# A background planner with other charges, later reads of products, and another split of score units between two engines

## The chip, the core and the metric

The kernel runs on one core of a Trainium2 chip. The core's engines run at the same time and each takes its own instructions in the order in which the program lists them: PE (TensorE, matrix products), DVE (VectorE), ACT (ScalarE), POOL (GpSimd) and SP (SyncE, which here only starts DMA transfers). An engine that reaches an instruction whose input is not ready stands still, and so does everything behind that instruction on the same engine. The metric is the device time of one execution in microseconds (us), lower is better; what is compared is the median of several runs.

## What is computed

One layer of attention with a kernel function of limited reach, then a mixture of experts, each between layer norms, on 4 sequences of 2048 tokens with 256 features, in float32:

```python
# attention: 16 heads of 16; z is one number for each head and token
out_i = sum_j max(0, 1 - |z_i - z_j| / b_h) * v_j          # j over 2048 keys
x = x + layernorm(attention(layernorm(x)) / T)
# experts: 64 experts, the best 8 for each token, at most 128 tokens for an expert
gu = h @ shared_gate_up_w                                   # h = layernorm(x)
shared = silu(gu[:, :512]) * gu[:, 512:] @ shared_down_w * sigmoid(h @ shared_gate_w)
w, idx = top_k(softmax(h @ gate_w), 8)
y = sum over the 8 of  w * (silu(h @ G_e) * (h @ U_e)) @ D_e
x = x + layernorm(y + shared)
```

The reference sorts the z values and uses prefix sums; the kernel forms the sum over j directly, as a matrix product.

## The kernel before

**The foreground** is a loop over 1024 score units (4 batches x 16 heads x 16 key tiles of 128). `score(t)` (L1535) makes one tile `hat` of 128 keys x 2048 queries: the absolute difference of a query row `qb` and a key column `nk`, then the minimum with 1, less 1. The second step is always DVE's (L1553). The first is ACT's (L1549), or, in a unit "on DVE alone", two further DVE instructions (L1544 and L1546). Which it is, is decided while the program is written out, by a running account `spare`: a unit on ACT adds to it, a unit on DVE alone and every background step on DVE subtract, and once it is 1.3 or more the next unit goes to DVE alone. `product(t)` (L1570) multiplies four quarters of the tiles of units t, t-1, t-2 and t-3 with the values on PE (L1579) and accumulates in the PSUM banks `pa`. After that the `hat` buffer is given back; `hat`, `qb` and `ct` share 13 buffers called big.

**The background** is everything else: preparing the next batch's norms, projections and values (`prepare`, L401), the rest of the attention layer, the shared expert and the routing of a finished batch (`finish`, L452), and, from about unit 700, the 64 experts for the tokens of the first two batches (`all_experts`, L980; `expert`, L1022). Each is written as small tasks with an engine, a charge in us, dependencies, and buffers that it takes and puts back. `Background.step` (L82) is called once after each score unit and writes out the tasks that are ready, engine by engine, until the sum of charges reaches that engine's cap for one unit (`CAP`); what was charged over the cap is carried as a debt. A task counts as ready some units after the tasks that it depends on (`LAG`): a DVE task one unit after a PE task, an ACT task four. So the charges, caps and lags set where a background instruction stands between the score units on its engine, and nothing is reordered afterwards.

**An expert** gathers up to 128 tokens (L1026, POOL, from the table `tab_d`), transposes them on PE (L1032), copies them (L1039, DVE), multiplies (L1036, PE), applies Silu (L1043, ACT), multiplies (L1044, DVE), multiplies with the down weights (L1046, PE), scales (L1049, DVE) and scatters with addition (L1051, POOL). Its weights come by two SP transfers (L987, L989) into one of three buffers called half: `h0`, `h1` and one of the ten slots `s0` to `s9`. Its tokens and results lie in a further slot.

**The tail.** After the last unit the planner runs alone (`drain`): the last batch's attention output and routing (`front_last`, `first` L704, `merge`, `ranking` with L1150), the two remaining batches' experts in 15 items (L1204 to L1243), what the loop left of the background, and the final norms of all 16 chunks (`final`, L1277 to L1309). Those finals for the first two batches wait for the last scatter of the first 64 experts.

Of the kernel before, what the change touches and what calls it, by code (L numbers as in the profile page):

```python
# [17 lines left out]
class Task:  # L18
    __slots__ = ("eng", "cost", "fn", "deps", "get", "put", "env", "lat", "at")

    def __init__(self, eng, cost, fn, deps, get, put, env, lat):
        self.eng, self.cost, self.fn, self.deps, self.lat = eng, cost, fn, deps, lat
        self.get, self.put, self.env, self.at = get, put, env, None


class Background:
# [6 lines left out]
    CAP = {"pe": 0.78, "dve": 0.65, "act": 0.30, "pool": 1.5, "sp": 2.0}  # L33
# [15 lines left out]
    def lag(self, d, k):  # L49
        if not self.alone:  # L50
            return self.LAG.get((d.eng, k.eng), 0) if d.lat is None else (d.lat + 3) // 2
        if d.lat is not None:
            return d.lat
        if d.eng == "sp":
            return 0 if k.eng == "sp" else 4
        return 0 if d.eng == k.eng else 1 if d.cost <= 0.7 else 2
# [25 lines left out]
    def step(self):  # L82

        self.t += 1
        full = set()
        cap = dict.fromkeys(self.CAP, 1.0) if self.alone else self.CAP
        for e, c in cap.items():
            self.debt[e] = max(0.0, self.debt[e] - c)
        left = []
        for k in self.q:  # L90
            if k.eng not in full and self.debt[k.eng] >= cap[k.eng]:
                full.add(k.eng)
            if k.eng not in full and self.ready(k, True):
                self.emit(k)
                self.debt[k.eng] += k.cost
            else:
                left.append(k)
        self.q = left
# [41 lines left out]
def sandwich_kernel(ctx: ExitStack, tc: tile.TileContext, x_in, wqT, bq, wkT, bk, wvT, bv, wprojT, log_bw,  # L140
# [84 lines left out]
    with ExitStack() as ph:  # L225
# [14 lines left out]
        def make(tag):  # L240
            uid[0] += 1
            if tag.startswith("s"):
                return sl.tile([P, SLW], F32, tag=tag, name=f"{tag}_{uid[0]}")
            if tag.startswith("pa"):
                return acc.tile([P, BK], F32, tag=tag, name=f"{tag}_{uid[0]}")
            if tag.startswith("h"):
                return wpool.tile([P, T // 2], F32, tag=tag, name=f"{tag}_{uid[0]}")
            if tag.startswith("v"):
                return vp.tile([P, NP, VW], F32, tag=tag, name=f"{tag}_{uid[0]}").rearrange("p a w -> p (a w)")
            if tag.startswith("b"):  # L250
                return bigp.tile([P, T], F32, tag=tag, name=f"{tag}_{uid[0]}")
            return ps.tile([P, BK], F32, tag=tag, name=f"{tag}_{uid[0]}")

        bg = Background(make)
# [32 lines left out]
        def norm_tasks(env, c, src, dst, deps, tag):  # L287

            st = small.tile([P, CH, 6], F32, tag=f"st{tag}{c}", name=f"st{tag}{c}_{uid[0]}")
            mv = small.tile([P, CH, 2], F32, tag=f"mv{tag}{c}", name=f"mv{tag}{c}_{uid[0]}")  # L290
            rs = small.tile([P, CH], F32, tag=f"rs{tag}{c}", name=f"rs{tag}{c}_{uid[0]}")

            def stats(i):
                for j in (i, i + 1):
                    nc.vector.bn_stats(st[:, j, :], src()[:, j, :])

            def scale():
                for j in range(CH):
                    nc.vector.bn_aggr(mv[:, j, :], st[:, j, :])
                nc.vector.tensor_scalar_add(rs, mv[:, :, 1], EPS)  # L300
                nc.gpsimd.tensor_tensor(out=rs, in0=rs, in1=mhalf, op=ALU.pow)  # L301

            def norm(i):
                for j in (i, i + 1):
                    nc.vector.tensor_scalar(dst()[:, j, :], src()[:, j, :], mv[:, j, 0:1], rs[:, j:j + 1],
                                            ALU.subtract, ALU.mult)
            a = [bg.add("dve", 0.75, lambda i=i: stats(i), deps) for i in (0, 2)]
            s = bg.add("dve", 0.6, scale, a)
            w = bg.add("pool", 0.0, lambda: None, [s])
            return [w], norm  # L310

        def transpose_tasks(env, src, dst, deps, key):

            done, reads = [], []
            for k in range(KF):
# [8 lines left out]
                a = bg.add("pe", 0.9, tr, deps, get={kk: "bank"}, env=env)  # L324
                done.append(bg.add("dve", 0.68, ev, [a], put=[kk], env=env))
# [9 lines left out]
        def values(env, c, done, dst, prev=None, b=None):  # L335
# [3 lines left out]
            for i2 in range(2):  # L339
# [17 lines left out]
                m0 = bg.add("pe", 0.95, lambda f=mmv: f(0), done, get={pk: "bank"}, env=env)  # L357
                m1 = bg.add("pe", 0.95, lambda f=mmv: f(1), [m0])
                e0 = bg.add("dve", 0.45, lambda f=evv: f(0), [m0, prev])
                e1 = bg.add("dve", 0.45, lambda f=evv: f(1), [m1, e0], put=[pk], env=env)  # L360
# [40 lines left out]
        def prepare(b, after=(), mdeps=()):  # L401
# [8 lines left out]
            for c in range(NCH):  # L410
# [6 lines left out]
                n_ = [bg.add("dve", 0.85, lambda i=i, f=norm: f(i), w) for i in (0, 2)]  # L417
# [10 lines left out]
            for r in range(R):  # L428
# [5 lines left out]
                for k in range(KF):  # L434
# [11 lines left out]
                    zz = bg.add("pe", 1.1, mmz, xts + [ld, zz], get={pz: "bank"} if zz is None else {}, put=put,  # L446
# [5 lines left out]
        def finish(b, after=()):  # L452
# [6 lines left out]
            def front(c):  # L459
# [15 lines left out]
                for i2 in range(2):  # L475
# [32 lines left out]
                    a = bg.add("pe", 0.9, tr, [free_pc, ld], get={pk: "bank"},  # L508
# [3 lines left out]
                    free_pc = bg.add("dve", 0.85, res, [w, ld], put=[pk], env=env)  # L512
# [4 lines left out]
                n_ = [bg.add("dve", 0.85, lambda i=i, f=norm: f(i), w) for i in (0, 2)]  # L517
# [27 lines left out]
                a = bg.add("pe", 1.4, mml, done, get={pl: "bank"}, env=env)  # L545
# [6 lines left out]
            def shared(c):  # L552
# [7 lines left out]
                for f in range(NI):  # L560
# [12 lines left out]
                    a = bg.add("pe", 1.1, lambda p_=pg, o=f * P, mm=mm: mm(p_, o, 0), done + [a], get=get, env=env)  # L573
                    g1 = bg.add("pe", 1.1, lambda p_=pg, o=f * P, mm=mm: mm(p_, o, 1), [a])
                    a = bg.add("pe", 1.1, lambda p_=pu, o=IS + f * P, mm=mm: mm(p_, o, 0), [g1])
                    a = u1 = bg.add("pe", 1.1, lambda p_=pu, o=IS + f * P, mm=mm: mm(p_, o, 1), [a],
# [3 lines left out]
                    ms.append(bg.add("dve", 0.68, lambda pu=pu, av=av: nc.vector.tensor_tensor(av(), av(), env[pu],  # L580
# [4 lines left out]
                for i2 in range(2):  # L585
# [17 lines left out]
                    a = bg.add("pe", 0.95, lambda f=mmy: f(0), ms + [a], get=get, env=env)  # L603
                    a = bg.add("pe", 0.95, lambda f=mmy: f(1), [a])
                    e0 = bg.add("dve", 0.45, lambda f=evy: f(0), [a, gts])
                    a = bg.add("pe", 0.95, lambda f=mmy: f(2), [a])
                    a = bg.add("pe", 0.95, lambda f=mmy: f(3), [a], put=acts if i2 == 1 else [], env=env)
# [10 lines left out]
            def tail():  # L618
# [29 lines left out]
                for i in range(0, NT, 4):  # L648
                    a = bg.add("dve", 0.6, lambda i=i: rep(i), [a])
# [13 lines left out]
                for r in range(NT // 8):  # L663
# [7 lines left out]
                    t_ = bg.add("pe", 0.9, tr, [a], get={pk: "bank"}, put=["lg"] if r == NT // 8 - 1 else [], env=env)  # L671
# [308 lines left out]
        def all_experts(env, a, half, out):  # L980

            gs = []
            for e in range(E):
                w = ("ew", e)

                def load(e=e, w=w):
# [9 lines left out]
                               [v(0, TW), v(TW, F), v(TW + F, P), v(TW + F + P, F)],  # L996
                               [{es: "slot"}, {}, {}], [[], [], [es]],
# [4 lines left out]
        def early(a, ready):  # L1002

            def bind():
# [8 lines left out]
                bg.free["half"] = [("h0", bg.t), ("h1", bg.t), bg.free["slot"].pop(0)]  # L1013
            env = {}
            a = bg.add("dve", 0.0, bind, [a] + last[B - 1]["v"] + last[B - 1]["z"])
# [6 lines left out]
        def expert(env, e, half, iv, deps, w, gu, dw, wkey, bufs, get, put, wcol):  # L1022
# [15 lines left out]
            a = bg.add("pe", 0.45, tr, [g], get={pt: "bank"}, env=env)  # L1038
            a = bg.add("dve", 0.42, lambda: nc.vector.tensor_copy(xT(), env[pt][:, :F]), [a], get=get[1],  # L1039
                       put=[pt], env=env)  # L1040
            a = bg.add("pe", 0.68, lambda: up(0), [a, w], get={pg: "bank"}, env=env)
            u = bg.add("pe", 0.68, lambda: up(1), [a])
            a = bg.add("act", 0.3, lambda: nc.scalar.activation(sg(), env[pg][:, :P], AF.Silu), [a])  # L1043
            a = bg.add("dve", 0.3, lambda: nc.vector.tensor_tensor(sg(), sg(), env[pg][:, P:2 * P], ALU.mult), [a, u],  # L1044
                       put=[pg], env=env)
            a = bg.add("pe", 0.74, lambda: nc.tensor.matmul(env[po][:, :F], lhsT=sg(), rhs=dw(),  # L1046
                                                           start=True, stop=True), [a], get={po: "bank"},
                       put=put[0] + ([wkey] if wkey else []), env=env)
            a = bg.add("dve", 0.48, lambda: nc.vector.tensor_scalar(og(), env[po][:, :F], wcol(xg()), None, ALU.mult), [a],  # L1049
# [278 lines left out]
        def norm_x0(c):  # L1328
            xv = lambda: chunkview(env0["x", c])
            w, norm = norm_tasks(env0, c, xv, xv, [], "a")  # L1330
            n_ = [bg.add("dve", 0.85, lambda i=i, f=norm: f(i), w) for i in (0, 2)]
            done, reads = transpose_tasks(env0, xv, lambda: featview(env0["xT", c]), n_, ("pt", c))
            bg.add("pe", 0.0, lambda: None, reads, put=[("x", c)], env=env0)
            xt0.append(done)
# [118 lines left out]
        def accumulate(g, r0, nr, k, deps, zz, st):  # L1453

            pz = ("pz", g)
            for r in range(r0, r0 + nr):
# [6 lines left out]
                zz = bg.add("pe", 0.6, mmz, deps + [zz], get={pz: "bank"} if zz is None else {}, env=env0)  # L1463
# [71 lines left out]
        def score(t):  # L1535
# [7 lines left out]
            if spare[0] >= 1.3:  # L1543
# [3 lines left out]
                spare[0] -= 3.7  # L1547
            else:
                nc.scalar.activation(ht, qb[n][0], AF.Abs, bias=k)  # L1549
                spare[0] += 1.92 - 1.23  # L1550
# [4 lines left out]
        def evict(t):  # L1555

            for c in range(4):
                if t - 1 - c >= 0 and (t - 1 - c) % UG == UG - 1:
# [6 lines left out]
                    spare[0] -= 0.7  # L1565
# [24 lines left out]
        with tc.manual_schedule():  # L1590
            for n in range(4):
                load_q(n)
            for t in range(B * NU + 5):
# [27 lines left out]
                if u == 0 and b == B - 2:  # L1621
                    bg.CAP = dict(bg.CAP, pe=0.88, dve=0.8, act=0.4)
# [144 lines left out]
```

## Time and profile before

| | us |
|---|---|
| median of 3 runs | 2415.87 |
| lowest, highest | 2414.73, 2419.77 |
| the profiled execution | 2422.47 |
| its span, first to last instruction | 2420.7 |
| preparation, to the first L1553 | 67.7 |
| 1024 score units, to the end of the last L1553 | 67.7 to 2105.9 |
| tail | 314.8 |

In the profile's groups, a row names the line, the engine, the operation, output and inputs, and the count; then the total busy time, the mean length of one in ns, and the idle time of the engine just before them with what ended it. Two instructions on ACT may overlap at their ends, so busy time divided by count is less than the mean length. In a row of waits the engine and its line stand first, then what it waited for, and then the total in us, the number of times and the longest. Where a table is cut by score stages here, a stage is 64 units, from the start of one L1553 to the start of the 64th after it.

### The profile page before, as it was taken

How to read it: one execution, taken by the hardware profiler on the slowest of the kernel's cores; microseconds unless marked ns; L12 is line 12 of the kernel's file. 1: busy time of each engine (PE TensorE's matmuls, PEld its weight loads, DVE VectorE, ACT ScalarE, POOL GpSimd, SP SyncE). 2: the span in 40 equal slices, each digit the busy share in tenths (PEclk: the TensorE clock that was granted, in tenths of full speed). 3: DMA queues.
4: the chain of work that ended last, by engine and by line, in shares of the span. 5: the costliest groups of instructions: out<-in, count | busy, mean ns of one | idle time of the engine just before them, and what ended most of it. 6: DMA issues, size and time to landing. Idle time of an engine off the chain costs nothing. (4 is left out here: it accounts for less than half of the span.)

```text
span 2420.7 us, 33022 instructions
## 1 busy us (share of the span) xinstructions
PE 1985.7 (82%) x12649; PEld 706.4 (29%) x12649; DVE 1971.5 (81%) x3064; ACT 2012.9 (83%) x1304; POOL 476.4 (20%) x326
## 2 busy tenths in 40 slices
PE   7686888897887888898898978778888878877785
PEld 4231222222222222222322212223233222353643
DVE  4597989998889988999989987878788789878344
ACT  2688999999989999999999999899799899742123
POOL 1000000100002100002100013454434444432432
PEclk9899999999999999999999999999899999998687
DMA  5223352444452312132312033554534443353872
GB/s 162 70 71 100 105 180 64 162 136 153 163 173 90 113 44 83 51 120 85 98 36 79 9 110 84 146 156 105 139 85 112 130 125 88 89 185 123 226 210 73
DMA packets 194871, 274.33 MB, mean 113 GB/s; under 512 B 24624, under 2 KB 165296, under 8 KB 193936
## 3 DMA queue, kind: packets, MB, share of 16 engines
q1 hardware_dynamic: 179536, 248.83, 32.2%
q0 software_dynamic: 15168, 23.31, 5.7%
q8 instruction: 101, 1.65, 0.3%
q14 instruction: 66, 0.54, 0.1%
HBM read 195.47 MB, written 76.61 MB: 112 GB/s over the span
## 5 line engine op out<-in xcount | busy, mean ns | idle before, releaser
L1549 ACT ACTIVATE hat<-qb,nk 128x2048 f32<-128x2048 f32 x978 | 1873.7, 1996 | 116.9 <-DMA qb<-zq_d 61.4
L1579 PE MATMUL pa<-hat,v 128*32 128x512 f32 x8192 | 1116.5, 618 | 327.3 <-DVE hat L1553 317.0
L1553 DVE TENSOR_SCALAR hat<-hat 128x2048 f32<-128x2048 f32 x1024 | 1232.2, 1224 | 118.3 <-ACT hat L1549 113.3
L1579 PEld LDWEIGHTS pa<-hat,v 128*32 128x32 f32 x8192 | 181.5, 109 | 921.5 <-DVE hat L1553 711.7
L1051 POOL DMA_INDIRECT y_d<-s,ix x64 | 154.1, 2407 | 254.3 <-DVE s L1049 173.4
L564 PE MATMUL k<-s,sgu 128*128 128x512 f32 x348 | 196.0, 648 | 0.0
L1026 POOL DMA_INDIRECT s<-tab_d,ix x64 | 113.6, 1775 | 373.4 <-DMA qb<-zq_d 243.5
L301 POOL TENSOR_TENSOR rsa<-rsa,mhalf 128x4 f32<-128x4 f32 x16 | 27.6, 1725 | 579.6 <-DVE rsa L300 562.8
L495 POOL TENSOR_TENSOR rsc<-rsc,mhalf 128x2 f32<-128x2 f32 x24 | 45.7, 1904 | 460.5 <-DVE rsc L494 460.3
L438 PE MATMUL k<-s,s 128*32 128x512 f32 x768 | 103.2, 604 | 0.0
L593 PE MATMUL k<-sd,s 128*128 128x256 f32 x352 | 97.3, 406 | 0.0
L564 PEld LDWEIGHTS k<-s,sgu 128*128 128x128 f32 x348 | 53.8, 192 | 129.4 <-issue 118.1
L593 PEld LDWEIGHTS k<-sd,s 128*128 128x128 f32 x352 | 62.2, 193 | 64.8 <-issue 47.4
L346 PE MATMUL k<-h,s 128*128 128x256 f32 x256 | 74.8, 418 | 0.0
L1036 PEld LDWEIGHTS k<-s,h 128*128 128x128 f32 x360 | 48.4, 201 | 52.7 <-issue 48.9
L704 DVE MAX8 codes<-scT 128x8 f32<-128x1152 f32 (+2 forms) x48 | 63.5, 1323 | 0.2
L346 PEld LDWEIGHTS k<-h,s 128*128 128x128 f32 x256 | 45.3, 196 | 57.8 <-issue 53.9
L1036 PE MATMUL k<-s,h 128*128 128x128 f32 x360 | 59.6, 302 | 2.0 <-issue 2.0
L1296 ACT ACTIVATE b<-b,v 128x256 f32<-128x256 f32 x64 | 33.2, 590 | 33.3 <-DVE v L1291 12.9
L1544 DVE TENSOR_SCALAR hat<-qb,nk 128x2048 f32<-128x2048 f32 x46 | 58.9, 1280 | 0.0
L1546 DVE TENSOR_SCALAR hat<-hat 128x2048 int32<-128x2048 int32 x46 | 56.5, 1228 | 1.6
L706 DVE MATCH_REPLACE8 scT<-codes,scT 128x1152 f32<-128x1152 f32 (+2 forms) x44 | 57.8, 1313 | 0.0
(305 smaller groups left out, 1674.1 us busy)
## 6 DMA issues: line engine op xcount, KB each, us to landing
qb<-zq_d SPq DMA_DIRECT2D x128, 512.0 KB, 6.2
s<-m_d SPq DMA_DIRECT2D x48, 512.0 KB, 4.2
s<-_attn_hidden_states_dram SPq DMA_DIRECT2D x28, 512.0 KB, 5.9
b<-y_d SPq DMA_DIRECT2D x24, 512.0 KB, 7.9
h<-fn_expert_gate_up_w_dram SPq DMA_DIRECT2D x45, 256.0 KB, 3.0
v_d<-h SPq DMA_DIRECT2D x48, 192.0 KB, 1.9
v<-v_d SPq DMA_DIRECT2D x48, 192.0 KB, 2.4
out_dram<-b SPq DMA_DIRECT2D x16, 512.0 KB, 3.9
```

The costliest lines, as they stand in the source:

```text
L346: nc.tensor.matmul(env[pk][:, i * F:(i + 1) * F], lhsT=xv[:, k, o:o + P], rhs=wv[:, k, :], start=(k == 0), stop=(k == KF - 1))
L438: nc.tensor.matmul(env[pz][c * CR:(c + 1) * CR, :], lhsT=xv[:, r, :], rhs=env[mp][:, k * 2 * F:(k + 1) * 2 * F], start=(r == 0 and k == 0) ...
L564: nc.tensor.matmul(env[p_], lhsT=sgu[:, k, o:o + P], rhs=featview(env[xT])[:, k, :], start=(k == 0), stop=(k == KF - 1))
L593: nc.tensor.matmul(env[py][:, i * F:(i + 1) * F], lhsT=env[acts[f // 2]][:, o:o + P], rhs=sd[:, f, :], start=(f == 0), stop=(f == NI - 1))
L704: a = bg.add("dve", 1.25, lambda c8=c8: nc.vector.max(out=c8, in_=scT[:, :w]), ev + [a])
L1026: g = bg.add("pool", 1.3, lambda: nc.gpsimd.indirect_dma_start(out=xg(), out_offset=None, in_=tab_d[half][:, :], in_offset=bass.IndirectOf ...
L1036: nc.tensor.matmul(env[pg][:, m * P:(m + 1) * P], lhsT=gu(k, m), rhs=xT()[:, k * P:(k + 1) * P], start=(k == 0), stop=(k == KF - 1))
L1051: s = bg.add("pool", 1.9, lambda: nc.gpsimd.indirect_dma_start(out=y_d[half][:, :], out_offset=bass.IndirectOffsetOnAxis(ap=iv(), axis=0), ...
L1544: nc.vector.tensor_scalar(ht, qb[n][0], k, None, ALU.add)
L1549: nc.scalar.activation(ht, qb[n][0], AF.Abs, bias=k)
L1553: nc.vector.tensor_scalar(ht, ht, 1.0, 1.0, ALU.min, ALU.subtract)
L1579: nc.tensor.matmul(pa[k, c][32 * j:32 * j + 32, :], lhsT=vt[b, s].rearrange("p a w -> p (a w)")[:, h // 2 * VW + p * D:h // 2 * VW + p * D ...
```

## The change

Six things are edited.

- The charges of many tasks are set to other numbers: transposes on PE go from 0.9 to 0.6 or 0.58, a step of the query and key projection from 1.1 to 0.88, a value product from 0.95 to 1.1, the router's product from 1.4 to 1.9, a down product of the shared expert from 0.95 to 1.07, and so on.
- The caps: PE 0.78 becomes 0.84 for the first two batches; in the last two PE stays at 0.88, and DVE goes from 0.8 to 0.75.
- A task that PE leaves with a debt over 0.65 is marked late, and whatever depends on it is written out one unit later.
- The account of `spare` gets other numbers.
- The tokens and results of one of the 64 early experts lie in half a slot, four halves made of two slots that are taken for good; three of the four small tiles of an expert now lie over one another.
- The buffers for these experts' weights are `h0`, `h1` and two slots that are taken for good, four instead of three.

```diff
-    CAP = {"pe": 0.78, "dve": 0.65, "act": 0.30, "pool": 1.5, "sp": 2.0}
+    CAP = {"pe": 0.84, "dve": 0.65, "act": 0.30, "pool": 1.5, "sp": 2.0}
...
         if not self.alone:
-            return self.LAG.get((d.eng, k.eng), 0) if d.lat is None else (d.lat + 3) // 2
+            return self.LAG.get((d.eng, k.eng), 0) + d.late if d.lat is None else (d.lat + 3) // 2
...
                 self.emit(k)
                 self.debt[k.eng] += k.cost
+                k.late = int(k.eng == "pe" and self.debt["pe"] > 0.65)
...
+            if tag.startswith("e"):
+                return ess[int(tag[1:]) // 2][:, int(tag[1:]) % 2 * (SLW // 2):]
...
+        NES, ess = 4, []
...
-                a = bg.add("pe", 0.9, tr, deps, get={kk: "bank"}, env=env)
-                done.append(bg.add("dve", 0.68, ev, [a], put=[kk], env=env))
+                a = bg.add("pe", 0.6, tr, deps, get={kk: "bank"}, env=env)
+                done.append(bg.add("dve", 0.63, ev, [a], put=[kk], env=env))
...
-                    zz = bg.add("pe", 1.1, mmz, xts + [ld, zz], get={pz: "bank"} if zz is None else {}, put=put,
+                    zz = bg.add("pe", 0.88, mmz, xts + [ld, zz], get={pz: "bank"} if zz is None else {}, put=put,
                                 env=env)
...
                 es = ("es", e)
                 v = lambda o, n, es=es: lambda: env[es][:, o:o + n]
...
-                               [v(0, TW), v(TW, F), v(TW + F, P), v(TW + F + P, F)],
-                               [{es: "slot"}, {}, {}], [[], [], [es]],
+                               [v(0, TW), v(0, F), v(TW, P), v(0, F)], [{es: "es"}, {}, {}], [[], [], [es]],
...
-                bg.free["half"] = [("h0", bg.t), ("h1", bg.t), bg.free["slot"].pop(0)]
+                bg.free["half"] = [("h0", bg.t), ("h1", bg.t), env["tag", "wq"][1:] + (bg.t,), env["tag", "wr"][1:] + (bg.t,)]
+                ess[:] = [env["e", i] for i in range(NES // 2)]
+                bg.free["es"] = [(f"e{i}", bg.t) for i in range(NES)]
             env = {}
-            a = bg.add("dve", 0.0, bind, [a] + last[B - 1]["v"] + last[B - 1]["z"])
+            get = {("e", i): "slot" for i in range(NES // 2)}
+            a = bg.add("dve", 0.0, bind, [a] + last[B - 1]["v"] + last[B - 1]["z"], get=dict(get, wq="slot", wr="slot"), env=env)
...
             if spare[0] >= 1.3:
                 nc.vector.tensor_scalar(ht, qb[n][0], k, None, ALU.add)
                 hi = ht.bitcast(I32)
                 nc.vector.tensor_scalar(hi, hi, 0x7fffffff, None, ALU.bitwise_and)
-                spare[0] -= 3.7
+                spare[0] -= 3.6
             else:
                 nc.scalar.activation(ht, qb[n][0], AF.Abs, bias=k)
-                spare[0] += 1.92 - 1.23
+                spare[0] += 1.9 - 1.17
...
-                    spare[0] -= 0.7
+                    spare[0] -= 0.63
...
-                    bg.CAP = dict(bg.CAP, pe=0.88, dve=0.8, act=0.4)
+                    bg.CAP = dict(bg.CAP, pe=0.88, dve=0.75, act=0.4)
```

The charges that the diff leaves out here, old and new: statistics of a norm 0.75 and 0.67, their scaling 0.6 and 0.47, applying a norm 0.85 and 0.68, a value's eviction 0.45 and 0.35, the first batch's projection step 0.6 and 0.43, the shared expert's gate and up products 1.1 and 1.05, its product on DVE 0.68 and 0.62, four masks of the routing 0.6 and 0.78, and within an expert 0.45 and 0.38 (L1032), 0.42 and 0.38 (L1039), 0.68 and 0.6 (L1036), 0.3 and 0.2 (L1044), 0.74 and 0.65 (L1046), 0.48 and 0.45 (L1049).

## The prediction

> **What bounds the kernel now.** I read the engine totals first, then the costliest groups, then busy times cut at every 64th score unit (the start of each 64th L1553), then the waits.
>
> ```profile
> span 2420.7 us, 33022 instructions
> PE 1985.7 (82%) x12649; PEld 706.4 (29%) x12649; DVE 1971.5 (81%) x3064; ACT 2012.9 (83%) x1304; POOL 476.4 (20%) x326
> ...
> L1549 ACT ACTIVATE hat<-qb,nk 128x2048 f32<-128x2048 f32 x978 | 1873.7, 1996 | 116.9 <-DMA qb<-zq_d 61.4
> L1579 PE MATMUL pa<-hat,v 128*32 128x512 f32 x8192 | 1116.5, 618 | 327.3 <-DVE hat L1553 317.0
> L1553 DVE TENSOR_SCALAR hat<-hat 128x2048 f32<-128x2048 f32 x1024 | 1232.2, 1224 | 118.3 <-ACT hat L1549 113.3
> ...
> L1544 DVE TENSOR_SCALAR hat<-qb,nk 128x2048 f32<-128x2048 f32 x46 | 58.9, 1280 | 0.0
> L1546 DVE TENSOR_SCALAR hat<-hat 128x2048 int32<-128x2048 int32 x46 | 56.5, 1228 | 1.6
> ```
>
> PE, DVE and ACT stand within two points of each other, so the shares alone choose no bound. Busy divided by count does: a unit with an ACT absolute value costs ACT 1873.7/978 = 1.916 us; every unit costs DVE 1232.2/1024 = 1.203 us; a unit on DVE alone costs DVE 1.280 + 1.228 = 2.508 us more and ACT nothing.
>
> The windows (length; then PE, PEld, DVE, ACT, POOL busy; clock; DMA) show where each limits. The first five are score stages 0, 1, 5, 9 and 12 of 16, the last is the tail:
>
> ```profile
> 67.70:207.60 139.90, 114.11 (x868) 41.75 (x868) 104.90 (x106) 112.65 (x59) 0.00 (x0) 0.95 0.22 70
> 207.60:328.90 121.30, 97.80 (x702) 30.30 (x698) 107.68 (x150) 114.23 (x61) 7.60 (x4) 0.96 0.35 117
> ...
> 682.80:802.40 119.60, 96.44 (x720) 25.79 (x724) 104.92 (x142) 115.47 (x64) 14.98 (x12) 0.96 0.44 136
> 1184.00:1314.40 130.40, 119.57 (x676) 34.40 (x672) 116.23 (x174) 128.98 (x78) 2.65 (x1) 1.00 0.16 53
> 1569.20:1710.00 140.80, 114.65 (x734) 38.90 (x734) 113.67 (x186) 125.14 (x79) 61.04 (x38) 0.93 0.55 148
> ...
> 2105.90:2420.70 314.80, 233.33 (x917) 150.25 (x916) 176.50 (x566) 89.24 (x177) 102.23 (x92) 0.82 0.53 157
> ```
>
> In stages 1, 5 and 9 ACT is busy for 94 to 99% of the time: ACT is the loop's bound. In stages 0 and 12 nothing is: those stages pay for waits. The loop ends at 2106; the tail takes 314.8 us, with ACT at 28%.
>
> What ACT, then DVE, waits for between 67.7 and 2105.9:
>
> ```profile
> ACT hat L1549 <- PE pa L1579: 49.0, 46, 4.2
> ACT hat L1549 <- DMA qb<-zq_d: 37.1, 23, 5.2
> ACT s L1043 <- PE k L1036: 33.3, 22, 6.1
> ...
> DVE hat L1553 <- ACT hat L1549: 113.3, 157, 6.6
> DVE s L1049 <- PE k L1046: 29.8, 27, 3.4
> DVE s L598 <- PE k L593: 27.4, 29, 2.1
> DVE s L1039 <- PE k L1032: 21.9, 24, 3.5
> ```
>
> The first line is ACT out of free hat buffers; the third is an expert's Silu standing on ACT before its product is done, with score units queued behind it. DVE's waits on a background product come to about 140 us with the smaller rows (L351 27.0, L540 14.3 and others).
>
> **More units on DVE alone.** In the order of the two built programs, 46 such units become 65. ACT loses 19 x 1.916 = 36.4 us and DVE gains 19 x 2.508 = 47.7 us. To see which engine then limits, I added busy/count of every ACT and DVE instruction standing between the marks of 64 units (ACT, DVE; stages 0 to 15):
>
> before ACT 111 115 115 107 117 113 129 126 126 132 126 117 125 121 124 127, sum 1930.5
> before DVE 109 114 110 106 113 113 119 115 124 117 117 104 121 110 118 117, sum 1824.9
> after ACT 111 111 113 111 111 127 120 116 121 127 127 112 121 128 123 115, sum 1893.9
> after DVE 114 113 120 117 111 123 115 112 121 120 117 108 124 124 120 112, sum 1869.7
>
> The larger of the two, unrounded, summed over stages: 1930.5 before, 1914.5 after. So 16.0 of ACT's 36.6 us survive; in stages 0 to 3, 8 and 12 DVE becomes the larger. Over groups of 8 units the same sum gives 1976.5 and 1972.9: only 3.6 us, if four to six hat buffers cannot average over more. The bounds are thus 36.6 and 3.6; I take 16.0, because stages 6 to 10 before ran within 2.4 us of their 64-unit load.
>
> What stages take beyond that load, before: 28.8 us in stage 0; 30.2 in stages 1 to 10, which hold 27 alone units, so 1.1 us for each; 48.6 in the expert stages 11 to 15 (13 alone units, 14.3 at that rate, and 34.3 left, near the 33.3 of Silu on L1036). After: stage 0 the same (6 alone units in both); stages 1 to 10 have 38 alone units, 42; stages 11 to 15 have 21, 23, plus what is left of the Silu wait.
>
> **Late products read one unit later.** In the built orders, 221 DVE reads stand one unit behind a product that leaves PE over 0.65 in debt; after, none does, and 65 of 100 ACT reads stand five units behind instead of four. A unit is 2 us and the mean Silu wait 33.3/22 = 1.5 us, so most go; I leave 8 of 33.3 (bounds 0 and 33.3). What gets late instead is the bank: it is freed a unit later, and PE's next task needs one of four. PE waits 317.0 us on hat already, so I charge nothing; without that cover, a bank would hold PE one unit at a time.
>
> Loop: 1914.5 + 28.8 + 42 + 23 + 8 = 2016, against 2038 now: -22 us.
>
> **Charges and caps.** These add no instruction; they move tasks. Adding background PE row times by stage: stage 0 stays at 57, stage 1 goes from 42 to 58, 5 from 40 to 62, 7 from 54 to 13, 15 from 49 to 61. With the products at 0.9 us a unit (stage 1: 97.8 - 42.2 = 55.6 over 64; stage 7, which is busy 115.05: 61 over 64) PE reaches 115, 119 and 119 in stages 1, 5 and 15, still at or under the larger load. I charge nothing; the second rival prices this.
>
> **Half buffers.** 64 gathers, 64 scatters and 128 weight loads remain; 13 experts' two loads move from the h buffers to ones made of score-stage slots. SP's and POOL's queues keep their counts (994 and 472 instructions). Four experts could be under way before; four can now. On SP a weight load moves past at most three qb loads (the first experts', which go behind them); ACT's 37.1 us on qb is left as it is, and each of its 23 waits, 1.6 us in the mean, is the price of one load pushed late.
>
> *A rule against it.* In-loop gathers (L1026) average 1775 ns against 1053 ns in the tail (L1204), scatters (L1051) 2407 against 1587 (L1243). The Trainium skill, "SBUF — State Buffer", section "Who interferes with whom", says that a VectorE tensor_scalar in a two-port mode and GpSimd exclude each other for a whole instruction. By that rule the 8 further alone units in stages 11 to 15 could hold POOL for 20 us, an estimate, and unhidden the sum below would be +6. By the rows alone, 16 more instructions x 0.77 (mean of the two differences) make 12 us, and unhidden the sum would be -2. POOL is busy 46 to 61 us of some 130 in each of those stages, so I charge nothing.
>
> **Tail.** 25 background steps fewer leave in the loop: about three experts more remain, two shared-expert steps fewer. Three experts cost POOL 3 x (1.775 + 2.407) = 12.5 us, and the first half's finals wait for the last scatter (at 2148 now). Those finals share the big buffers with the ranking of the last batch: in the built order L1150's step comes later, and the last add too. Bounds 0 (PE idles 81 of 315 us) and 12.5; I take 8, since a buffer handed on late delays the whole chain.
>
> Sum: -22 + 8 = -14. The profiled execution took 2422.47, span 2420.7, so a span near 2407. Its median sibling is 2415.87, so **2402 us**.
>
> **Rivals.**
> A, forecast, 50%: 2402, own range 2390 to 2411, from the bounds of Silu, tail and the 1.1 us.
> B, 13%: reading late also frees PE and ACT remains the only bound. All 36.6, Silu's 33.3 halved, no loss in the tail: -53, 2363. For it: DVE's 140 us of waits on products are three times its new load. Against: six stages in which DVE now has more to do.
> C, 22%, slower: PE takes over where tasks were drawn forward. Place: stages 1 and 5, with PE at 115 and 119, and ACT and DVE above 110, as stage 0 is now. Price: stage 0's 21.1 us of ACT waiting for hat buffers, in place of the 6.6 and 3.3 I charged: +32, so -14 + 32 = +18, 2434. It decides once ACT's wait on L1579 rises from 49 over 65 us. Against: stage 9 has PE at 119.6 and loses nothing.
> D, 15%: no change worth the name: the balance over 8 units holds (3.6, its finer sum containing the waits of alone units), Silu gives 10, and the tail takes 12.5: -1, 2415. This is also the case in which the change doesn't do what it says.
>
> **Numbers.** One measurement of this kernel can tell about 0.2% (4.8 us) from no change. Faster: A but for 2 points, and B, 0.61; the same: D and those 2 points, 0.17; slower: C, 0.22. The range goes from two thirds of the way to B, 2376, to C's 2434.
>
> **What would show it.** L1549 x959 and L1544 x65; loop end near 2084 instead of 2106; Silu L1043 waiting under 10 us; the tail from 315 to about 323. I'd be wrong at the late reads if ACT's wait on L1036 stays above 20; at the balance if DVE's idle time behind ACT stays at 113 with the loop no shorter; at the charges if the wait on L1579 grows past 65.

## The result and the profile after

| | before | after |
|---|---|---|
| median, us | 2415.3 | 2378.5 |
| runs | 2411.3 to 2419.8 | 2377.1 to 2381.3 |
| span of the profiled execution | 2420.7 | 2376.8 |
| preparation | 67.7 | 66.3 |
| 1024 score units | 2038.2 | 1996.9 |
| tail | 314.8 | 313.6 |

The change makes the kernel faster: the ratio is 0.9841 with a 95% interval of 0.9815 to 0.9867, so -37 us at the medians. The forecast was 2402. The two profiled executions differ by 43.9 us; 41.3 of them lie in the loop, and the tail keeps its length (-1.2 us). Line numbers move by 4 to 6: the score's ACT line is L1555 now, its DVE lines are L1550, L1552 and L1559, the product is L1585.

These are the engine totals and the same groups of the changed kernel's page:

```profile
span 2376.8 us, 32919 instructions
PE 1987.5 (84%) x12649; PEld 721.6 (30%) x12649; DVE 2008.0 (84%) x3102; ACT 1977.6 (83%) x1285; POOL 477.1 (20%) x326
...
L1555 ACT ACTIVATE hat<-qb,nk 128x2048 f32<-128x2048 f32 x959 | 1839.5, 1996 | 135.3 <-PE pa L1585 64.2
...
L1550 DVE TENSOR_SCALAR hat<-qb,nk 128x2048 f32<-128x2048 f32 x65 | 83.1, 1278 | 0.6 <-DMA qb<-zq_d 0.5
```

ACT gave up 35 us and DVE took 36.5 us more in total; DVE is now the busiest engine of all. The busy times of score stages 0, 1, 5, 9 and 12 and of the tail, in the columns used before:

```profile
66.30:196.60 130.30, 113.55 (x870) 41.12 (x870) 108.91 (x127) 111.56 (x59) 3.29 (x2) 0.95 0.26 84
196.60:316.20 119.60, 109.03 (x832) 37.60 (x824) 109.78 (x135) 112.53 (x60) 5.62 (x3) 0.96 0.44 148
680.00:812.10 132.10, 118.08 (x692) 34.97 (x692) 115.50 (x212) 128.02 (x79) 14.64 (x11) 0.97 0.32 99
1173.30:1302.60 129.30, 120.74 (x680) 34.67 (x679) 119.15 (x169) 126.49 (x77) 0.00 (x0) 0.99 0.18 61
1552.30:1680.50 128.20, 103.92 (x740) 37.71 (x732) 115.58 (x182) 118.53 (x77) 65.44 (x36) 0.99 0.58 163
2063.20:2376.80 313.60, 242.41 (x952) 162.72 (x951) 179.63 (x574) 90.18 (x180) 110.17 (x98) 0.80 0.56 162
```

Stage 0 has as many units on DVE alone as before (six), nearly the same PE and ACT time and 4 us more of DVE, and is 9.6 us shorter: what went is waiting. Stage 12 is 12.6 us shorter. Stage 5 is 12.5 us longer, because work was drawn forward into it: ACT is busy for 128.0 us there instead of 115.5, and idle for 4.1 us in both kernels. The waits of ACT and then of DVE in the loop:

```profile
ACT hat L1555 <- PE pa L1585: 64.2, 55, 3.3
...
ACT s L1049 <- PE k L1042: 11.1, 9, 2.7
...
DVE hat L1559 <- ACT hat L1555: 101.1, 122, 6.5
DVE s L602 <- PE k L597: 23.2, 16, 3.4
DVE s L1055 <- PE k L1052: 15.4, 18, 3.0
DVE s L1045 <- PE k L1038: 14.5, 16, 4.5
```

Silu's wait on ACT fell from 33.3 to 11.1 us. DVE's waits on background products, all rows added, fell from 143 to 85.

### The profile page after: what moved, and what is told of

Same layout as the page of the kernel before. It is cut to its first block, busy times and chain, and to the rows that moved or that the text cites. A ratio compares the mean times of both kernels' runs of the same rounds, so it can differ in the third digit from the quotient of the medians.

```text
span 2376.8 us, 32919 instructions
## 1 busy us (share of the span) xinstructions
PE 1987.5 (84%) x12649; PEld 721.6 (30%) x12649; DVE 2008.0 (84%) x3102; ACT 1977.6 (83%) x1285; POOL 477.1 (20%) x326
## 5 line engine op out<-in xcount | busy, mean ns | idle before, releaser
L1555 ACT ACTIVATE hat<-qb,nk 128x2048 f32<-128x2048 f32 x959 | 1839.5, 1996 | 135.3 <-PE pa L1585 64.2
L1585 PE MATMUL pa<-hat,v 128*32 128x512 f32 x8192 | 1126.3, 626 | 300.5 <-DVE hat L1559 287.9
L1559 DVE TENSOR_SCALAR hat<-hat 128x2048 f32<-128x2048 f32 x1024 | 1229.4, 1222 | 107.2 <-ACT hat L1555 101.1
L1585 PEld LDWEIGHTS pa<-hat,v 128*32 128x32 f32 x8192 | 189.7, 110 | 917.9 <-DVE hat L1559 661.0
L1057 POOL DMA_INDIRECT y_d<-s,ix x64 | 149.8, 2341 | 301.9 <-DVE s L1055 161.2
L1032 POOL DMA_INDIRECT s<-tab_d,ix x64 | 106.0, 1656 | 319.2 <-DMA qb<-zq_d 255.9
L499 POOL TENSOR_TENSOR rsc<-rsc,mhalf 128x2 f32<-128x2 f32 x24 | 55.4, 2310 | 512.9 <-DVE rsc L498 512.8
L1550 DVE TENSOR_SCALAR hat<-qb,nk 128x2048 f32<-128x2048 f32 x65 | 83.1, 1278 | 0.6 <-DMA qb<-zq_d 0.5
L1552 DVE TENSOR_SCALAR hat<-hat 128x2048 int32<-128x2048 int32 x65 | 79.8, 1228 | 2.2
L442 PEld LDWEIGHTS k<-s,s 128*32 128x32 f32 x768 | 32.4, 139 | 54.3 <-issue 54.2
L582 ACT ACTIVATE s<-k 128x512 f32<-128x512 f32 x45 | 26.3, 584 | 19.8 <-PE k L568 19.8
```

The lines of the kernel that those rows point to most:

```text
L442: nc.tensor.matmul(env[pz][c * CR:(c + 1) * CR, :], lhsT=xv[:, r, :], rhs=env[mp][:, k * 2 * F:(k + 1) * 2 * F], start=(r == 0 and k == 0) ...
L1032: g = bg.add("pool", 1.3, lambda: nc.gpsimd.indirect_dma_start(out=xg(), out_offset=None, in_=tab_d[half][:, :], in_offset=bass.IndirectOf ...
L1057: s = bg.add("pool", 1.9, lambda: nc.gpsimd.indirect_dma_start(out=y_d[half][:, :], out_offset=bass.IndirectOffsetOnAxis(ap=iv(), axis=0), ...
L1550: nc.vector.tensor_scalar(ht, qb[n][0], k, None, ALU.add)
L1552: nc.vector.tensor_scalar(hi, hi, 0x7fffffff, None, ALU.bitwise_and)
L1559: nc.vector.tensor_scalar(ht, ht, 1.0, 1.0, ALU.min, ALU.subtract)
```

## The experiments

All were timed against the kernel before, whose median lay between 2413.8 and 2420.3 in them; so a difference between the medians of two experiments is good to some 6 us. Behind each time stand its ratio to the kernel before and the ratio's 95% interval. The sums of waits named below are over the loop, in one profiled execution each. In the four whose names hold "split" the list of units on DVE alone is written out instead of chosen by the account; the background does not depend on it, so that only the part named differs.

**The split of units kept from the other kernel.** `after_split46` is the changed kernel with the old 46 units on DVE alone, `before_split65` the kernel before with the new 65:

```diff
-            if spare[0] >= 1.3:
+            if t in ALONE:
```

> The changed kernel, with its background unchanged, but with the 46 units of the kernel before on DVE alone in place of its own 65. Theory S (the loop is ACT's load and the split is worth all of it): ACT gets back 19 x 1.916 = 36 us, so about 2378 + 30 to 36 = 2408 to 2414, and the loop's length grows by as much. Theory R (the one on record, the split is worth 16 us less its own waits): 2378 + 0 to 10. Theory L (reading late is most of the gain, the split little): 2378 + 0 to 12 as well, so L and R are told apart by the run without late reads.

> The kernel before, with the 65 units of the changed kernel on DVE alone and nothing else changed. Theory S: 2415 - 30 to 36 = about 2382. Theory R: 2415 - 16 + 21 of waits for 19 more such units = about 2415 to 2420. Theory L: DVE already loses some 140 us to products that it reads too early, so 47.7 us more on it makes it the bound: 2420 to 2440.

Measured: 2433.9 (ratio 1.0092, 1.0065 to 1.0119) and 2507.6 (1.0405, 1.0380 to 1.0430). Every theory missed, and in both directions at once: each list is good in its own kernel and costs 55 or 94 us in the other. What follows is that the place of these units matters far more than their number. A list made for another background puts 2.5 us of DVE where DVE is already full, and leaves ACT its 1.9 us where ACT is full. Sums of row durations agree: add up, in the order written out, each row's busy time divided by its count over groups of 16 units, and take the larger of ACT's and DVE's load in each group. With the 46 kept this sum is some 80 us larger than in the changed kernel, and the loop is 58 us longer (2055.0); with the 65 in the kernel before it is some 65 us larger, and the loop is 80 us longer (2118.0). So pinned lists cannot price the split, and the account has to choose for itself.

**Without the late mark**, first with the 65 units kept, then with the account choosing (64 units):

```diff
-            return self.LAG.get((d.eng, k.eng), 0) + d.late if d.lat is None else (d.lat + 3) // 2
+            return self.LAG.get((d.eng, k.eng), 0) if d.lat is None else (d.lat + 3) // 2
```

> The changed kernel without the late mark (products read one unit earlier again), with its 65 units on DVE alone kept. Theory L: most of the gain goes, 2400 to 2415, and ACT's wait for the up product of an expert (L1042 in the changed kernel) is back at about 33 us from 11. Theory S: 2378 to 2385. Theory R: 2378 + 25 (Silu) = about 2400.

> The changed kernel without the late mark, its own account choosing the units on DVE alone again (64 of them, at other places than in the run with the 65 kept). Theory P (place: the kept units stood where DVE had no room, and that made the run 107 us slower): the account repairs most of it, 2378 + 5 to 20. Theory L (reading a late product one unit later is itself worth tens of us, because DVE and ACT stand behind PE with score units queued after them): 2378 + 40 to 100, with stage 0 at about 148 us as in the run with the units kept, against 130.

Measured: 2485.2 (1.0299, 1.0273 to 1.0324), which no theory had, and 2435.4 with the account's own choice (1.0063, 1.0038 to 1.0088), where theory L had it. The choice repairs 50 us of 107; the other 57 (54 by the ratios) are the late mark's. All that the change does, without its late reads, is slower than the kernel before. The loop takes 2060.9 us instead of 1996.9. DVE's waits on background products are 170 us and ACT's on products 54; the largest rows of ACT and DVE, apart from DVE's wait on the score's ACT half:

```profile
ACT hat L1554 <- PE pa L1584: 75.4, 61, 4.7
ACT s L1048 <- PE k L1041: 50.7, 28, 4.4
...
DVE s L1044 <- PE k L1037: 38.8, 27, 5.5
DVE s L1054 <- PE k L1051: 35.4, 38, 2.8
DVE s L601 <- PE k L596: 25.4, 25, 1.6
DVE v L354 <- PE k L349: 21.9, 7, 5.1
```

How it works is seen on DVE's timeline just after the loop's start. In this kernel a value's eviction (L354, which takes the product out of its bank) stands too close behind its product; DVE waits for it, and the score units queued behind wait too:

```profile
69.71 1.23 DVE L1558 TENSOR_SCALAR hat<-hat 128x2048 f32<-128x2048 f32 x1 [1.92 <-ACT hat L1554]
74.79 0.42 DVE L354 TENSOR_TENSOR v<-k,h 128x256 f32<-128x256 f32 x1 [3.85 <-PE k L349]
75.14 1.22 DVE L1558 TENSOR_SCALAR hat<-hat 128x2048 f32<-128x2048 f32 x1
...
84.26 0.42 DVE L354 TENSOR_TENSOR v<-k,h 128x256 f32<-128x256 f32 x1 [3.86 <-PE k L349]
84.60 1.22 DVE L1558 TENSOR_SCALAR hat<-hat 128x2048 f32<-128x2048 f32 x1
```

The same stretch of the changed kernel, where the eviction comes one unit later and finds its product done, or nearly so:

```profile
73.32 1.23 DVE L1559 TENSOR_SCALAR hat<-hat 128x2048 f32<-128x2048 f32 x1
74.46 0.42 DVE L355 TENSOR_TENSOR v<-k,h 128x256 f32<-128x256 f32 x1
77.05 1.23 DVE L1559 TENSOR_SCALAR hat<-hat 128x2048 f32<-128x2048 f32 x1 [2.17 <-ACT hat L1555]
78.19 0.41 DVE L355 TENSOR_TENSOR v<-k,h 128x256 f32<-128x256 f32 x1
78.94 1.23 DVE L1559 TENSOR_SCALAR hat<-hat 128x2048 f32<-128x2048 f32 x1 [0.34 <-ACT hat L1555]
80.49 0.42 DVE L355 TENSOR_TENSOR v<-k,h 128x256 f32<-128x256 f32 x1 [0.32 <-PE k L350]
```

**Which reader it is.** The late mark is heeded by DVE's reads alone, or by ACT's alone:

```diff
-            return self.LAG.get((d.eng, k.eng), 0) + d.late if d.lat is None else (d.lat + 3) // 2
+            return self.LAG.get((d.eng, k.eng), 0) + (d.late if k.eng == "dve" else 0) if d.lat is None else (d.lat + 3) // 2
```

> The changed kernel with the late mark heeded by DVE's reads alone; ACT's Silu reads stay four units behind. Without any late reads the kernel takes 2435, with all 2378.5. Theory D (what counts is DVE, which stands behind a product with score units queued after it: 172 us of such waits without late reads, 85 with): 2378 + 0 to 15. Theory A (what counts is ACT's Silu, 54 us of waits without, 11 with): 2378 + 35 to 57, with ACT's wait on the up product above 30 us. By the changes in waits, 87 to 43, a share of two thirds to DVE: about 2397.

> The changed kernel with the late mark heeded by ACT's reads alone; DVE's reads are one unit behind again. Theory D: 2435 - 0 to 20 = 2415 to 2435, with DVE's waits on background products at about 170 us. Theory A: 2378 to 2400. By shares of the waits: about 2416.

Measured: 2395.9 (0.9887, 0.9858 to 0.9917) with DVE alone heeding it, 2417.3 (0.9987, 0.9972 to 1.0001) with ACT alone. Against 2435 that is 40 us by DVE's reads and 18 by ACT's, near the 57 of both together and near the shares of their waits. But this sum holds by luck, since it mixes loop and tail. Here are the waits in the loop, in us:

| late mark heeded by | ACT on products | ACT on hat buffers | ACT on query rows | DVE on products | loop | tail |
|---|---|---|---|---|---|---|
| none | 54 | 75 | 33 | 170 | 2060.9 | 310.8 |
| ACT's reads | 22 | 95 | 34 | 151 | 2042.5 | 310.1 |
| DVE's reads | 35 | 60 | 20 | 74 | 1994.7 | 332.6 |
| all: the changed kernel | 11 | 64 | 38 | 85 | 1996.9 | 313.6 |

DVE's reads alone bring the whole gain of the loop, and they shorten ACT's waits of all three kinds, though ACT's own reads stay four units behind their products. ACT's reads alone bring 18 us: most of what ACT no longer waits for products it then waits for hat buffers. With DVE alone it is the tail that is longer, by 19 us; 60 of the 64 gathers start in the loop instead of 62. One more part of the mark is in neither run: in the changed kernel a task on PE that depends on a late product stands a unit later too. As the loop is as short without it, nothing shows that it brings anything there.

**The account alone, and everything but the account.**

```diff
-                spare[0] -= 3.7
+                spare[0] -= 3.6
...
-                spare[0] += 1.92 - 1.23
+                spare[0] += 1.9 - 1.17
```

> The kernel before with the new numbers in the account alone: 57 units on DVE alone instead of 46, the background unchanged. Theory P: the larger load over 64 units goes from 1930.5 to 1916.2, so 2414 - 5 to 14 = 2400 to 2409. Theory L: as products are read early, more work on DVE brings nothing, 2414 +- 8 or slower.

> The changed kernel with the old numbers in the account of units on DVE alone: its background is unchanged, and the account chooses 54 instead of 65. Theory P: 11 units back on ACT cost at most 11 x 1.916 = 21 us and the larger load over 64 units goes from 1914.5 to 1921.5, so 2378 + 7 to 21. Theory L: the split is worth next to nothing, 2378 + 0 to 7.

Measured: 2418.5 with the new account in the kernel before (1.0015, 1.0000 to 1.0030; 56 such units in the trace), and 2374.0 with the old account in the changed kernel (0.9821, 0.9797 to 0.9845; 54 units). Its interval overlaps the changed kernel's, so in time the last eleven units bring nothing. Theory P was wrong. The loop of the old account, the loop of the changed kernel, and what ACT waits for with the old account:

```profile
67.70:2056.70 1989.00, 1687.07 (x11347) 524.03 (x11347) 1779.39 (x2398) 1889.96 (x1092) 350.96 (x194) 0.98 0.36 106
66.30:2063.20 1996.90, 1700.21 (x11344) 532.06 (x11345) 1800.33 (x2420) 1871.77 (x1081) 357.30 (x194) 0.96 0.35 106
ACT hat L1555 <- PE pa L1585: 45.4, 47, 3.2
...
ACT s L1049 <- PE k L1042: 2.6, 3, 2.3
```

The eleven units take 18 us from ACT's busy time in the loop and add 26 to its idle time: with DVE fuller by 21 us, ACT waits longer for hat buffers (64.2 instead of 45.4) and for products (11.1 instead of 2.6). The traces before and after alone would mislead here: between them ACT's busy time falls by 36 us (1908.0 to 1871.8) and its idle time by 5, as if the split had paid. (The profiled execution of the old account, 2371.7, was the fastest of its four; the medians differ by 4.5 us.)

**The buffers.** The changed kernel with a whole slot for each expert and three weight buffers again, first with the 65 units kept, then with its own choice:

```diff
-                               [v(0, TW), v(0, F), v(TW, P), v(0, F)], [{es: "es"}, {}, {}], [[], [], [es]],
+                               [v(0, TW), v(TW, F), v(TW + F, P), v(TW + F + P, F)],
+                               [{es: "slot"}, {}, {}], [[], [], [es]],
...
-                bg.free["half"] = [("h0", bg.t), ("h1", bg.t), env["tag", "wq"][1:] + (bg.t,), env["tag", "wr"][1:] + (bg.t,)]
+                bg.free["half"] = [("h0", bg.t), ("h1", bg.t), bg.free["slot"].pop(0)]
```

> The changed kernel with the old buffers for the early experts (a whole slot each for the tokens, three for the weights) and its 65 units on DVE alone kept. On record the buffers are worth nothing: 2378 +- 5. A rival: four weight buffers and slots of their own keep the experts evenly spread, so that without them fewer are done in the loop (58 instead of 62 have begun) and the tail gets longer by 4 experts x 2 to 4 us: 2386 to 2394, with all of it behind the last score unit.

> The changed kernel with the old buffers for the early experts, its own account choosing 65 units. Kept units gave 2430, of which 27 us in the loop (all of it in the last two stages) and 25 us in the tail, with 58 experts begun in the loop instead of 62. Theory P: the account repairs the loop's part, the tail stays 20 to 25 us longer: 2378 + 20 to 30. If the tail is back to 314 us, the buffers cost nothing and the kept units did it all.

Measured: 2429.8 (1.0058, 1.0035 to 1.0082), more than either expectation had, and 2401.2 (0.9934, 0.9908 to 0.9959), as theory P had it. With its own choice the loop is as long as in the changed kernel (1996.5 and 1996.9); the buffers are worth 23 us, and 21.5 of them are the tail's. Whether it is the fourth weight buffer or the halves taken for good is not shown, as both were put back at once. Loop and tail of that run:

```profile
67.40:2063.90 1996.50, 1686.17 (x11330) 525.04 (x11331) 1799.59 (x2413) 1870.22 (x1078) 344.18 (x188) 0.97 0.35 105
2063.90:2399.00 335.10, 255.14 (x967) 169.09 (x965) 185.89 (x580) 90.76 (x183) 121.02 (x103) 0.77 0.54 159
```

**Late reads and buffers with the old charges, then with the new charges and the old caps.** Both are the kernel before with these lines and the buffers of the change; the second has all the change's charges too, of which one is shown:

```diff
-            return self.LAG.get((d.eng, k.eng), 0) if d.lat is None else (d.lat + 3) // 2
+            return self.LAG.get((d.eng, k.eng), 0) + d.late if d.lat is None else (d.lat + 3) // 2
...
+                k.late = int(k.eng == "pe" and self.debt["pe"] > 0.65)
...
-                    zz = bg.add("pe", 1.1, mmz, xts + [ld, zz], get={pz: "bank"} if zz is None else {}, put=put,
+                    zz = bg.add("pe", 0.88, mmz, xts + [ld, zz], get={pz: "bank"} if zz is None else {}, put=put,
```

> The kernel before with the late mark and the new buffers for the early experts; charges, caps and account are the old ones (49 units on DVE alone, 56 experts begun in the loop). If late reads need the new charges to know what is late (theory C), the loop stays within 15 us of 2038. If they work by themselves (theory D), the loop is 1985 to 2005 and only the tail is longer, 8 experts x 5 us = 40, so 2380 to 2405.

> Late mark, new buffers and new charges; caps and account are the old ones (53 units on DVE alone, 63 experts begun). With the new caps as well it is the version that took 2374. If the caps are worth nothing: 2374 +- 5. If the higher PE cap for the first two batches crowds PE (stage 5 takes 132 us in every version that has it, against 120): the loop is 5 to 15 us shorter, 2360 to 2369. If the cap is what draws the background forward in time: 2380 to 2395.

Measured: 2417.3 (0.9988, 0.9974 to 1.0002) and 2362.3 (0.9756, 0.9732 to 0.9780). With the old charges the loop is 44.9 us shorter than before, and the tail gives all of it back, 361.8 us: 58 of the 64 gathers start in the loop, and ten scatters are left for the tail. With the new charges 63 gathers start in the loop, four scatters are left, and the tail is 310.1:

```profile
67.40:2060.70 1993.30, 1694.27 (x11291) 517.49 (x11291) 1763.77 (x2370) 1899.03 (x1094) 331.41 (x185) 0.97 0.35 105
2060.70:2422.50 361.80, 257.40 (x1004) 171.71 (x1004) 190.14 (x591) 88.19 (x182) 123.36 (x106) 0.78 0.52 149
```

```profile
67.40:2051.80 1984.40, 1698.11 (x11383) 527.85 (x11383) 1781.87 (x2403) 1892.17 (x1094) 361.39 (x196) 0.98 0.36 107
2051.80:2361.90 310.10, 233.43 (x913) 152.30 (x912) 175.35 (x566) 89.72 (x179) 106.74 (x95) 0.81 0.55 161
```

The first two lines are of the version with the old charges, the last two of the one with the new. The latter beats the changed kernel by 16 us; it is the fastest of this study. The late mark with the old buffers and charges was not run, nor the new charges without the late mark in the kernel before.

**The caps one by one, and an earlier mark**, all on top of that fastest version:

```diff
-    CAP = {"pe": 0.78, "dve": 0.65, "act": 0.30, "pool": 1.5, "sp": 2.0}
+    CAP = {"pe": 0.84, "dve": 0.65, "act": 0.30, "pool": 1.5, "sp": 2.0}
```

```diff
-                    bg.CAP = dict(bg.CAP, pe=0.88, dve=0.8, act=0.4)
+                    bg.CAP = dict(bg.CAP, pe=0.88, dve=0.75, act=0.4)
```

```diff
-                k.late = int(k.eng == "pe" and self.debt["pe"] > 0.65)
+                k.late = int(k.eng == "pe" and self.debt["pe"] > 0.4)
```

> Late mark, new buffers, new charges (that version took 2362) and PE's cap of 0.84 for the first two batches; DVE's cap for the last two stays at 0.8. Theory PE (crowding in the stages drawn forward, the slower rival on record): most of the 12 us between 2362 and 2374, so 2370 to 2376, lost in stages 3 to 6, with ACT's wait for hat buffers up. Theory DVE (the lower DVE cap leaves an expert less in the loop): 2362 +- 4.

> Late mark, new buffers, new charges and DVE's cap of 0.75 for the last two batches; PE's stays at 0.78. Theory PE: 2362 +- 4. Theory DVE: 2368 to 2376, lost after unit 512 and in the tail (62 experts begun in the loop instead of 63).

> The version that took 2362 with the mark set from a debt of 0.4 instead of 0.65, so that more products are read one unit later. If every read one unit behind PE is still too early, DVE's wait on background products falls from 74 us towards 50 and the loop gets 5 to 15 us shorter; but 58 experts are begun in the loop instead of 63, and with 58 the tail took 335 us instead of 310: 2372 to 2390 in all. If the tail does not follow the count of experts, 2347 to 2360.

Measured: 2371.4 (0.9796, 0.9776 to 0.9816) with PE's cap, 2370.2 (0.9789, 0.9768 to 0.9811) with DVE's, 2387.5 (0.9866, 0.9847 to 0.9885) with the mark from 0.4. Each cap alone costs some 8 to 9 us, in different places, so each theory names one half of the cost. PE's cap lengthens the loop by 11.6 us, 9.2 of them in stage 5. That is not the crowding which theory PE named: ACT waits for no hat buffer in stage 5 in either version, and 4.6 of the 9.2 us are more work on ACT there. DVE's lengthens the tail by 6.3 and the loop by 3.0. The earlier mark shortens the loop by 4.3 us more and the tail takes 341.1.

Set in order, one profile each, the parts of the change add up as follows:

| version | loop | tail |
|---|---|---|
| before | 2038.2 | 314.8 |
| + late mark and buffers | 1993.3 | 361.8 |
| + charges | 1984.4 | 310.1 |
| + caps | 1989.0 | 313.2 |
| + account: the changed kernel | 1996.9 | 313.6 |

These are steps in one order; another order could give other prices. And the tail against the scatters of early experts (L1051, L1057 after the change) that start after the loop's end:

| scatters left over | 0 | 2 | 4 | 5 | 7 | 8 | 8 | 10 |
|---|---|---|---|---|---|---|---|---|
| last one, us after the loop | none | 42 | 51 | 60 | 89 | 100 | 104 | 119 |
| tail, us | 310.8 | 314.8 | 310.1 | 313.6 | 332.6 | 335.1 | 341.1 | 361.8 |

The columns are the kernels without the late mark, before, fastest, after, DVE's reads alone, old buffers, earlier mark, old charges. The nine kernels that the table leaves out fit: 308.4 to 316.4 us with up to five left over, 338.4 with eight. Up to five left over show no cost; from five to ten the tail grows by (361.8 - 313.6)/5 = 9.6 us for each in the mean. The count stands for all that is left of the experts: the work on PE in the tail grows with it too, from 242 to 257 us.

## Why the prediction came out as it did

The direction was right and the size was not: -14 was forecast, -37 came.

*What bounds the loop*: right as far as ACT's load goes, but too narrow. The prediction read DVE's 140 us of waits on background products and left them to rival B. Those waits delay the score units queued behind them on DVE. Where DVE's reads alone come later, DVE's waits fall from 170 to 74 us, and ACT's for hat buffers from 75 to 60, for products from 54 to 35.

*Reading late*: the step that failed, by its size. The sentence was "A unit is 2 us and the mean Silu wait 33.3/22 = 1.5 us, so most go; I leave 8 of 33.3": 25 us, ACT's reads alone. Silu's wait did fall, to 11.1. But late reads are worth 57 us in the changed kernel, 64 in its loop, and DVE's reads alone bring all of those 64; ACT's alone bring 18. The loop is 45 us shorter where late reads are added with the buffers to the kernel before. The DVE reads were counted (221 that stood one unit behind) and given no price.

*More units on DVE alone*: the terms of the record add to nothing, -16 for the larger load and +21 for waits at 1.1 us a unit, so +5. The runs price eleven of the nineteen, the account's own: +7.9 in the loop of the traces and +4.5 at the medians, inside the noise. The sum was right as far as that goes, though the text named the split among the gains; the eight units that come with the rest of the change were not priced apart. The finer sum, over 8 units, came nearer to what the split is worth than the one over 64.

*Charges and caps*, charged at nothing: wrong. On top of late reads and buffers the charges bring 52 us in the tail and 9 in the loop; with them 63 gathers start in the loop instead of 58. The caps together cost 12 us.

*Half buffers*, charged at nothing: wrong, 21.5 us of tail. "Four experts could be under way before; four can now" was true of the limit that the order sets, but only three had weight buffers, and their slots were shared with the other batches' work; without the change 59 gathers start in the loop instead of 62. Which of the two counts is open.

*Tail*, +8 for three experts left over: three more scatters were left (five instead of two), but -1.2 was measured. Five late scatters cost nothing that shows, and L1150 even starts 10 us sooner after the loop's end (117 against 127). The bound of 12.5 is no bound beyond that: with seven to ten scatters left the tail is 19 to 48 us longer.

*The rivals.* B, 2363, was nearer than the forecast, but not for its reason: its 36.6 us of split never came. C, PE crowded where work is drawn forward, came in neither of its two places. Stage 1 went from 121.3 to 119.6. Stage 5 went from 119.6 to 132.1, but with no wait of ACT for hat buffers before or after: its 12.5 us are ACT's larger load, which the prediction's own list has (113 to 127), while stage 7 is 8.6 us shorter. ACT's wait on hat buffers did rise to 64.2 in all, just under the 65 that was to decide, but it rose in stages 2, 3, 11 and 15 above all (together from 3 to 26), and fell from 21 to 12 in stage 0; what raised it there is not shown. D did not happen.

*The rule against it*: in the loop gathers took 1676 ns and scatters 2404, less than the 1775 and 2433 before, with 19 more units on DVE alone. But there the whole background moved. With the changed kernel's background held, 46, 54 and 65 such units go with gathers of 1612, 1622 and 1676 ns and scatters of 2274, 2332 and 2404. That is the direction of the exclusion that the Trainium skill, "SBUF — State Buffer", section "Who interferes with whom", describes, though no run shows that it is the cause. From 46 to 65 it makes some 12 us of POOL, which is busy for 357 of the loop's 1997 us; a price in time was not seen, as was assumed.

*The signs*: the counts came (959 and 65). The loop ended at 2063 and not near 2084, Silu's wait was 11.1 and not under 10, the tail was 314 and not 323.

What stays open: how much of the 57 us the late mark would bring to the kernel before without the new buffers, and which part of the buffers counts.

## What to carry to other kernels

On an engine that works in order, everything queued behind a read that is placed too close behind its product waits too. So price such waits on every engine that feeds the bound, not on the bound alone: here DVE's later reads took 97 us off its waits and 66 us off the loop, though ACT was the bound. Reads placed later can leave more work over at the end, so ask how much is left, and from which count on it no longer hides. And where units may go to either of two engines, their place matters before their number: a list good in one schedule cost 55 to 94 us in another, while ten or eleven units more at places chosen for the schedule changed nothing clear of noise.

## What the runs showed that was not expected

The same order of instructions repeats its time closely: up to unit 704 the changed kernel and `nobuf_split65` have the same instructions in the same order, and their eleven stages differ by 0.0 to 2.0 us each. The mean granted clock of PE was a little lower after the change, 0.943 over the span against 0.954 before, although the kernel is faster.
